# The products with the adjacency matrix in float32r, x in two parts, and due times for each operation

## The chip, the cores and the metric

The kernel runs on one core of a Trainium2 chip. The metric is the device time of one execution in microseconds. A core has five engines that run side by side and meet at semaphores: TensorE (PE, matrix products; its weight loads are listed as PEld), VectorE (DVE), ScalarE (ACT), GpSimd (POOL) and SyncE (SP), which here issues all transfers. Matrix products write to PSUM banks, all else lies in SBUF.

## The reference

The input is 32 graphs of 512 nodes: `x` (32 x 512 x 256) and `adj` (32 x 512 x 512, entries 0 and 1, ones on the diagonal), both float32. Four layers follow one another, each with a residual and a layer norm. Cut to what matters:

```python
# layer 0: attention with 8 heads, masked by adj
scores = einsum('bhqd,bhkd->bhqk', q, k) / sqrt(HD)
scores = where(adj[:, None] > 0, scores, NEG)
x = layernorm(x + einsum('bhqk,bhkd->bhqd', softmax(scores), v) @ Wo + bo)
# layer 1: aggregate, then two dense layers of 512
h = (1.0 + eps) * x + einsum('bnm,bmd->bnd', adj, x)
x = layernorm(x + relu(h @ W1 + b1) @ W2 + b2)
# layer 2: aggregate, then two dense layers of 1024 with RMS norm and silu
agg = epsilon * x + einsum('bnm,bmd->bnd', adj, x)
h = agg @ W1 + b1
x = layernorm(x + silu(rmsnorm(h) * rms_weight) @ W2 + b2)
# layer 3: Laplacian of adj, scaled by the degrees
s_out, s_in = rsqrt(sum(adj, 1)), rsqrt(sum(adj, 2))
L = eye - s_out[:, :, None] * adj * s_in[:, None, :]
pre = xn @ W_self + einsum('bij,bjf->bif', L, xn) @ W_neigh
x = layernorm(x + softplus(pre))
```

So adj enters three large products with 256 columns of features: one in layer 1, one in layer 2 and one in layer 3.

## The kernel before

One graph is worked at a time in tiles of 128 nodes (NT = 4 tiles) and 128 features (DC = 2). `graph(b)` does not issue instructions. It describes each operation of graph b to a planner (`Order`): the engines that can do it with an estimated cost on each (in nanoseconds), the keys that it reads and writes, the buffers that it holds. When all 32 graphs are described, `emit` gives each operation a due time, which is the graph's number times `PERIOD` plus a value from an early and a late pass over one graph and a lead for its stage (`LEAD`), and then simulates the engines: at each step the ready operation with the smallest due time goes next on its engine. The order thus found is what each engine's queue holds; operations of two or three graphs stand mixed in it. Where an operation can go to two engines (`either`, `copy_either`, `evacuate`), the planner takes the one that ends first by its estimate.

The stages of a graph, with the names used later:

- `load`: x into `y_att` (L407), adj into `ad` (L410; one buffer, so the load of the next graph waits until the last use of this one).
- `adjT`: the transposed adj, two buffers. The first graph transposes `ad` on PE into PSUM (`pt_adj`, L605) and ACT copies it out, summing the rows for `d_out` on the way (L615). The others load adj a second time in runs of 32 elements with four transfers (`load_blocks`, L595), transpose the 32x32 blocks on DVE with two instructions (L629) and let ACT sum over each of four tiles in place (L639). `bias` on DVE (L653) makes the mask for the attention.
- `xT`, `qk`, `v`, `scores`, `move`, `pv`: the attention. PE writes the scores, DVE adds the mask and takes the maximum (L808), ACT takes the exponential (L822), DVE transposes blocks (L858), and the result goes out to DRAM (`via`) and back (`pT`). In the first graph PE does these transposes too (`pt_p`, L841). `pr_r` (L970) spreads the reciprocal sums with small bfloat16 products.
- `wo`, `degree`, `ln0`: output product; ACT sums adj for `d_in` (L1102); two chains of small operations make `s_out` and `s_in`; layer norm.
- `agg1`: `set_diagonal` on DVE (L1159) puts `diag0` (the diagonal of adj) plus the self weight on adjT's diagonal; `aggregate` (L1177) makes the product: for each of 2 feature tiles and 4 node tiles a float32 product of 128 x 128 by 128 x 512 columns, into a bank `ph`.
- `w11`, `w12`, `ln1`, `agg2`, `w21`, `rms`, `w22`, `ln2`: the dense layers, and the second aggregate. In `rms` DVE scales 8 tiles of gT (L1333) and ACT takes Silu in two halves (L1348). POOL adds the squares (`ssq`, L554).
- `x3T`, `pz`: x goes out and back through DRAM for its transpose; the product with both weights of layer 3 gives `zy` (its first half the self part, its second the neighbour part, which is scaled with `s_in`).
- `lap`: 4 x 4 float32 products of adjT with 256 columns of zy into `pa_l` (L1489), and a DVE operation per tile that scales by `ns_out` and adds (L1500).
- `softplus`, `ln3`: ACT makes Abs, Exp and Ln in a tile `sp`; POOL adds; layer norm; store.

Some tags are shared buffers: `aT` (one) holds the tile `aT` between `w11` and `w12`, and later `zy`; `sq` (one) holds the squares; `y` (three) holds the residuals and `sp`; `adjT` has two.

## Time and profile before

| what | us |
|---|---|
| three runs | 3340.52, 3337.96, 3341.30 |
| median | 3340.52 |
| span of the profiled execution, first to last instruction | 3336.2 |
| PE busy in it | 3284.9 |
| DVE busy | 2672.1 |
| ACT busy | 1958.3 |
| POOL busy | 842.5 |
| transfers, mean share of the 16 DMA engines | 73.4% |

The costliest groups that touch adjT, from the table of instructions (busy us, then the mean ns of one):

| group | count | busy | one |
|---|---|---|---|
| L1177 PE, both aggregates | 512 + 512 records | 230.4 + 227.4 | 603 and 596 |
| L1489 PE, Laplacian | 1024 records | 229.2 | 382 |
| L629 DVE, block transposes of adjT | 62 | 75.5 | 1238 |
| L639 ACT, row sums | 124 | 76.5 | 618 |
| L1102 ACT, column sums | 128 | 78.7 | 616 |
| L1159 DVE, set_diagonal | 64 | 43.3 | 676 |

PE's records overlap, since products are pipelined: the mean of one is longer than the distance between two. The distance is what counts, and it is read from a run of them in the order of time (length over number). One float32 product leaves two records. The transfers are listed by the instruction that issued them, with the time to landing.

### The profile page before, as it was taken

Reading aid. Unit: us, or ns where it says so; the run is one execution under the profiler, and the core shown is the slowest. Engines: PE = TensorE matmul, PEld = TensorE weight load, DVE = VectorE, ACT = ScalarE, POOL = GpSimd, SP = SyncE. Lnnn points to the kernel's source line nnn. Section 1 sums busy time; section 2 is a strip of 40 time slices with the busy share of each in tenths; the row PEclk is TensorE's granted clock in tenths of the full one; section 3 lists DMA queues with packets and bytes.
Section 4 is the critical chain, followed back from the end, with each engine's and each line's share of the span. In section 5 each row is a group of like instructions: output and inputs, shape, how many; then the busy total and the mean of one; then the engine's idle time right before and its main releaser. Section 6 shows DMA issues by size and latency. Waiting matters only on the chain.

```text
span 3336.2 us, 54850 instructions
## 1 busy us (share of the span) xinstructions
PE 3284.9 (98%) x19624; PEld 1980.4 (59%) x19624; DVE 2672.1 (80%) x6195; ACT 1958.3 (59%) x4062; POOL 842.5 (25%) x611
## 2 busy tenths in 40 slices
PE   8999999999999999999999999999999999999997
PEld 5456665566665566655566655666555666556654
DVE  8878887788887888887888878888878878778855
ACT  6555666566665656665665656666656556566534
POOL 1222222222222222222222222222222222222221
PEclk9999999999999999999999999999999999999999
DMA  6878777777777777786777877777877778777720
GB/s 152 249 223 230 199 207 221 200 227 211 203 216 226 199 219 210 208 227 196 222 212 204 214 226 198 223 203 213 223 210 211 217 199 216 224 197 217 197 44 26
DMA packets 768193, 677.21 MB, mean 203 GB/s; under 512 B 540208, under 2 KB 592304, under 8 KB 736176
## 3 DMA queue, kind: packets, MB, share of 16 engines
q1 hardware_dynamic: 767920, 673.71, 73.4%
q8 instruction: 155, 2.54, 0.3%
q14 instruction: 118, 0.97, 0.1%
HBM read 380.52 MB, written 293.08 MB: 202 GB/s over the span
## 4 chain that ended last, share of the span: by engine, by line
PE 93%; DVE 2%; DMA 2%; ACT 1%; SPq 1%; issue 0%; POOL 0%; POOLq 0%; DVEq 0%; ACTq 0%
PE po L998 22%; PE ph L1177 13%; PE pg L1194 12%; PE sc L784 8%; PE po_att L900 7%; PE pa_l L1489 7%; PE pa L1194 6%; PE pq L711 6%; PE pz L1443 6%; PE pv L752 3%; DMA via<-pq 1%; SPq L595 1%; ACT pq L822 1%; DVE pq L858 0%; DVE pq L808 0%
## 5 line engine op out<-in xcount | busy, mean ns | idle before, releaser
L822 ACT ACTIVATE pq<-pq,mx 128x512 f32<-128x512 f32 x1024 | 729.1, 713 | 307.0 <-DVE mx L808 279.1
L808 DVE CUSTOM_DVE_ANT_0 pq<-sc,bias 128x512 f32<-128x512 f32 x1024 | 664.6, 682 | 97.8 <-PE sc L784 87.6
L858 DVE STREAM_TRANSPOSE pq<-pq 128x2048 f32<-128x2048 f32 x248 | 569.7, 2298 | 148.8 <-ACT pq L822 147.7
L1194 PE MATMUL pg<-hT,w 128*128 128x512 f32 x1024 | 469.9, 598 | 0.2 <-DVE zy L1454 0.2
L998 PE MATMUL po<-w,gT 128*128 128x256 f32 x2048 | 448.6, 379 | 6.8 <-ACT gT L1348 6.8
L554 POOL TENSOR_TENSOR ssq<-ssq,sq 128x512 f32<-128x512 f32 x218 | 277.9, 1275 | 589.3 <-ACT sq L1270 589.3
L998 PEld LDWEIGHTS po<-w,gT 128*128 128x128 f32 x2048 | 388.7, 190 | 63.9 <-ACT gT L1348 9.6
L1051 POOL TENSOR_TENSOR rstd<-ve,nhalf 128x4 f32<-128x4 f32 (+1 forms) x132 | 134.5, 1020 | 843.3 <-DVE ve L1046 842.1
L1194 PEld LDWEIGHTS pg<-hT,w 128*128 128x128 f32 x1024 | 189.3, 190 | 261.3 <-issue 223.6
L784 PE MATMUL sc<-kT,qT 32*128 32x512 f32 x2048 | 291.9, 640 | 0.3 <-DVE mx L808 0.3
L900 PEld LDWEIGHTS po_att<-pT,v 128*32 128x32 f32 x8192 | 219.6, 110 | 49.8 <-DVE zy L1454 21.2
L1443 PE MATMUL pz<-wsn,xnT 128*128 128x512 f32 x512 | 240.2, 595 | 5.2 <-DVE s_in L1118 3.3
L900 PE MATMUL po_att<-pT,v 128*32 128x128 f32 x8192 | 237.3, 273 | 2.1 <-DMA pT<-via 2.1
L1177 PE MATMUL ph<-adjT,y_att 128*128 128x512 f32 x512 | 230.4, 603 | 0.0
L998 PE MATMUL po<-w,aT 128*128 128x256 f32 x1024 | 229.5, 382 | 0.0
L1489 PE MATMUL pa_l<-zy,adjT 128*128 128x256 f32 x1024 | 229.2, 382 | 0.0
L1194 PE MATMUL pa<-hT,w 128*128 128x512 f32 x512 | 228.3, 599 | 0.0
L1177 PE MATMUL ph<-adjT,y 128*128 128x512 f32 x512 | 227.4, 596 | 0.0
L998 PEld LDWEIGHTS po<-w,aT 128*128 128x128 f32 x1024 | 192.0, 190 | 48.4 <-issue 22.0
L1489 PEld LDWEIGHTS pa_l<-zy,adjT 128*128 128x128 f32 x1024 | 192.1, 190 | 26.4 <-issue 0.9
L822 ACT ACTIVATION_READ_ACCUMULATOR pq<-pq,mx 128x1 f32 x1024 | 192.3, 188 | 0.0
L1270 ACT ACTIVATE sq<-gT 128x512 f32<-128x512 f32 x224 | 140.0, 625 | 88.4 <-POOL ssq L554 44.2
(166 smaller groups left out, 4685.1 us busy)
## 6 DMA issues: line engine op xcount, KB each, us to landing
via<-pq SPq DMA_DIRECT2D x992, 256.0 KB, 5.0
pT<-via SPq DMA_DIRECT2D x248, 1024.0 KB, 6.7
adj<-in_adj_dram SPq DMA_DIRECT2D x32, 1024.0 KB, 8.3
adjT<-in_adj_dram SPq DMA_DIRECT2D x124, 256.0 KB, 6.7
y_att<-in_x_dram SPq DMA_DIRECT2D x32, 512.0 KB, 4.3
xT<-in_x_dram SPq DMA_DIRECT2D x124, 128.0 KB, 4.0
x3d<-y SPq DMA_DIRECT2D x31, 512.0 KB, 2.9
xnT<-x3d SPq DMA_DIRECT2D x124, 128.0 KB, 7.2
```

The costliest lines, as they stand in the source:

```text
L554: lambda: nc.gpsimd.tensor_tensor(dst(), dst(), src(), ALU.add), {},
L711: nc.tensor.matmul(pq(), lhsT=w[:, c, m * P : (m + 1) * P], rhs=xT[:, c, :], start=(c == 0), stop=(c == DC - 1),)
L784: nc.tensor.matmul(sc[:, j, :], lhsT=qT[hp, g, t * P : (t + 1) * P], rhs=kTs[g][hp, :], start=True, stop=True,)
L808: lambda t=t, j=j, sc=sc, row=row: nc.vector.tensor_tensor_reduce(out=row(), in0=sc[:, j, :].rearrange("p (a n) -> p a n", a=4), in1=bias[ ...
L822: lambda t=t, j=j, row=row: nc.scalar.activation(row(), row(), AF.Exp, bias=mx[:, t, j : j + 1], scale=-1.0, accum_out=rs[:, g, t, j : j + 1],
L858: lambda pq=pq: nc.vector.transpose(pq().rearrange("p a j c s -> p (a j c s)"), pq().rearrange("p a j c s -> p (a j c s)"),),
L900: nc.tensor.matmul(po[j * HD : (j + 1) * HD, t * P : (t + 1) * P], lhsT=v[:, c, h * HD : (h + 1) * HD], rhs=pTs[t][:, :, j, c, :], start=( ...
L998: nc.tensor.matmul(po[:, i * D : (i + 1) * D], lhsT=lhs[:, k, t * P : (t + 1) * P], rhs=w[:, k, :], start=(i == 0 and k == 0), stop=(i == ...
L1177: nc.tensor.matmul(ph(), lhsT=xin[:, m, c * P : (c + 1) * P], rhs=adjT[:, m, :], start=(m == 0), stop=(m == NT - 1),)
L1194: nc.tensor.matmul(pa(), lhsT=w[:, c, m * P : (m + 1) * P], rhs=hT[:, c, :], start=(c == 0), stop=(c == DC - 1),)
L1443: nc.tensor.matmul(pz(), lhsT=xnT[:, c, t * P : (t + 1) * P], rhs=wsn[:, c, :], start=(c == 0), stop=(c == DC - 1),)
L1489: nc.tensor.matmul(pa[:, at], lhsT=adjT[:, m, t * P : (t + 1) * P], rhs=zy[:, m, D : 2 * D], start=(m == 0), stop=(m == NT - 1),)
```

## The change

Six things change at once.

1. `adjT` becomes a float32r tile for every graph. The operand on the other side (x1, x2, or the scaled neighbour half of zy) is split by `parts_of` into a float32r copy (high) and the rest (low), also float32r: one operation each on DVE or ACT, and on DVE or POOL. `aggregate` then makes two products for each that it made before; the Laplacian's product has both parts side by side as 512 columns, and the two halves of the bank are scaled and added.
2. Whether the float32r copies of adj and of its changed diagonals are exact is checked on the chip: differences on POOL, their absolute sums on ACT into `inexact`, and after the last graph one sum and one small product into `found`. A register is loaded from it; if it is not zero, a loop does all graphs again in float32 (`general=True`, one graph at a time, in the order as written).
3. adj is transposed on PE in all graphs, not only in the first; the second load of adj and DVE's block transposes of it go.
4. The due times are a list with one number for each operation, in three lists (first graph, graphs between, last graph); the early and late passes go. A handicap of 1000 ns is added to DVE wherever an operation can go to several engines.
5. Work is moved between engines: the column sums of adj come early, into a scratch tile; the two degree chains become one on tiles twice as wide; `set_diagonal` is an addition on POOL and a copy on ACT or DVE; half of the RMS scalings go to POOL, and their Silu runs by tile; layer norm's last step can go to POOL.
6. Buffers: `y_att` takes one of the three `y` buffers, and its load waits for the residual `r2` of the graph before; `sp` goes, and softplus works in place in `zy`; the parts of x (`hl`) use the buffer of `aT`; the scratch tiles of the checks use that of `sq`.

The core of the diff:

```diff
-PERIOD = 68064
-LEAD = {
-    "adjT": 136800, "agg1": -11000, "agg2": -29700, "degree": 92400, "diag": 77700,
...
+AHEAD = 3
+PERIOD = 117877
+DUE = {
+    "first": [
+        -953, -1983, -977, -2779, -2566, -630, -2955, -2775, -1468, -707, -1979, -879, -867, -503,
...
+    HANDICAP = {"PE": 0, "DVE": 1000, "ACT": 0, "POOL": 0, "SP": 0}
...
-            for o, d in zip(lst, dues[len(lst)]):
-                keys[o.n] = b * period + d - (self.HASTE if b == max(by_b) else 0)
+            due = DUE["first" if b == 0 else "last" if b == max(by_b) else "middle"]
+            for o, d in zip(lst, due, strict=True):
+                keys[o.n] = b * period + 100 * d
...
-        y = tmp([P, NT, D], "y_att", 2)
+        y = tmp([P, NT, D], "y", 3, "y_att")
...
-            [], [(y, t) for t in range(NT)],
+            [("r2", b - 1)], [(y, t) for t in range(NT)],
...
-        adjT = tmp([P, NT, N], "adjT", 2)
...
-            for q in range(4):
-                op(
-                    [("SP", 2500, lambda q=q: load_blocks(adjT(), adj[b], q), {"issue": 1250})],
...
+        adjT = tmp([P, NT, N], "adjT", 2, dtype=F32 if general else F32R)
...
+        def differs(c, t, k, cost):
+            act(
+                cost,
+                lambda: nc.scalar.activation(t(), t(), AF.Abs, accum_out=inexact[:, b, c : c + 1]),
+                [], k + [("inexact", b, c)],
+            )
+
+        for m in range(NT):
+            pt = bank("pt_adj")
...
+            pe(460, tr_adj, [(ad, t) for t in range(NT)], [(pt,)], adjT, d_out)
+            act(
+                860,
+                lambda m=m, pt=pt: nc.scalar.activation(
+                    adjT[:, m, :], pt(), AF.Identity, accum_out=d_out[:, m : m + 1]
+                ),
+                [(pt,)], [(adjT, m), (d_out, m)],
+            )
...
+            if not general:
+                pool(
+                    1280,
+                    lambda t=t, same=same: nc.gpsimd.tensor_tensor(
+                        ad[:, t, :], ad[:, t, :], same().bitcast(F32), ALU.subtract
+                    ),
+                    [(same,)], [(ad, t)],
+                )
...
+        def set_diagonal(selfI, self_k, c):
+            t = tmp([P, NT, P], "sq", 1, "diag")
+            pool(
+                1280,
+                lambda: nc.gpsimd.tensor_tensor(
+                    t(), diag0(), selfI.unsqueeze(1).to_broadcast([P, NT, P]), ALU.add
+                ),
+                [(diag0,), (self_k,)], [(t,)],
+            )
+            copy_either(lambda: diagonal(adjT()), t, [(t,)], allT)
...
+        def parts_of(src, src_k, dst, dst_k):
+            high = lambda e: e.tensor_copy(dst(0), src())
+            low = lambda e: e.tensor_tensor(dst(1), src(), dst(0).bitcast(F32), ALU.subtract)
+            op(
+                [
+                    ("DVE", 300, lambda: high(nc.vector), {"port": 1}),
+                    ("ACT", 420, lambda: nc.scalar.copy(dst(0), src()), {}),
+                ],
+                src_k, [dst_k(0)],
+            )
+            op(
+                [
+                    ("DVE", 350, lambda: low(nc.vector), {}),
+                    ("POOL", 690, lambda: low(nc.gpsimd), {}),
+                ],
+                src_k + [dst_k(0)], [dst_k(1)],
             )
...
+            if not general:
+                hl = tmp([P, 2, NT, D], "aT", 1, "hl", dtype=F32R)
+                for t in range(NT):
+                    parts_of(
+                        lambda t=t: xin[:, t, :], [(xin, t), ("lapped", b - 2)],
+                        lambda r, t=t: hl[:, r, t], lambda r, t=t: (hl, r, t),
+                    )
...
+                            for r in range(1 if general else 2):
+                                src = xin[:, m] if general else hl[:, r, m]
+                                nc.tensor.matmul(
+                                    ph(),
+                                    lhsT=src[:, c * P : (c + 1) * P],
+                                    rhs=adjT[:, m, :],
...
+        whole = C2 if general else C2 // 2
+        if whole < C2:
+            pb_s = tmp([P, N], "sq", 1, "pb_s")
+            evacuate(pb_s, pb, [(pb,)], [(pb_s,)])
         for m in range(C2):
+            if m >= whole:
+                pool(
+                    1280,
+                    lambda m=m: nc.gpsimd.tensor_tensor(gT[:, m, :], gT[:, m, :], pb_s(), ALU.mult),
...
+                    nc.tensor.matmul(
+                        pa[:, 0:D] if general else pa(),
+                        lhsT=adjT[:, m, t * P : (t + 1) * P],
+                        rhs=zy[:, m, D : 2 * D] if general else yhl[:, m].rearrange("p r d -> p (r d)"),
...
+    any_found = nc.values_load(found[0:1, 0:1], min_val=0, max_val=1)
+    with tc.If(any_found != 0):
+        with tc.For_i(0, B, 1) as i:
+            one = Order()
+            parts = [v[bass.ds(i, 1)].rearrange("o n d -> (o n) d") for v in (x, adj, out)]
+            graph(0, one, *parts, general=True)
```

## The prediction, made before the changed kernel was run

> **What bounds the kernel now.** I read the page's busy shares and its forty slices first.
>
> ```profile
> PE 3284.9 (98%) x19624; PEld 1980.4 (59%) x19624; DVE 2672.1 (80%) x6195; ACT 1958.3 (59%) x4062; POOL 842.5 (25%) x611
> ...
> PE   8999999999999999999999999999999999999997
> ...
> PEclk9999999999999999999999999999999999999999
> ```
>
> TensorE (PE) works in every slice at the full granted clock; only the first and last slices dip. A busy PE may still wait, so I looked at one graph's period in the table of stretches and in the chain of waits:
>
> ```profile
> 578.67:680.32 101.65, 101.65 (x610) 61.20 (x609) 82.74 (x193) 61.19 (x128) 26.56 (x20) 1.00 0.79 213
> 1304.00:1405.66 101.66, 101.66 (x610) 61.22 (x609) 82.67 (x192) 61.32 (x128) 26.57 (x19) 1.00 0.78 213
> ```
>
> The columns are length, then busy time of PE, weight loads, DVE, ACT and POOL. The steady period is 101.66 us, PE has no hole in it, and DVE has 19 us, ACT 40 us, POOL 75 us to spare. 32 periods are 3253 us; the other 83 us of the 3336.2 us span are its two ends. The chain of the second stretch is PE alone:
>
> ```profile
> 1312.20 7.07 PE ph L1177 x16
> ...
> 1342.04 0.45 PE pr_r L970 x8
> 1342.49 6.92 PE ph L1177 x16
> ...
> 1377.57 7.00 PE pa_l L1489 x32
> ```
>
> So a microsecond taken from PE here shortens the period, until another engine or a buffer stops it. The three products with adj (aggregate twice, the Laplacian once) cost 7.07 + 6.92 + 7.00 = 20.99 us.
>
> **The change, part by part.**
>
> *The products.* A float32 product leaves two PE records: ph's 8 products are 16 records of 0.442 us, pa_l's 16 products are 32 records of 0.219 us at half the columns. So a record streams at two steps a column, a float32 product at four. pr_r's bf16 products, one record each, take 0.45/8 = 0.056 us for 128 columns: one step. No float32r product is in the trace. After the change each stage has 16 products of 512 columns (two parts times eight in aggregate; 16 with both parts side by side in the Laplacian), 48 a graph. Bounds for one: 512 bf16-like columns, 4 x 0.056 = 0.225 us; one record of float32, 0.442; a whole float32 product, 0.884. I take 0.222, between the bf16 figure and the 0.219 of a record with equally many steps: splitting x into parts that are exact in a narrower format means one pass over a shorter mantissa, which the bf16 row is nearest to. The weight load must hide: it is 0.190 us for pa_l's records and does so under 0.219. 48 x 0.222 = 10.66 us; saved 10.33 a graph, 330.6 us in all.
>
> *adj transposed on PE.* The first graph already does this; the other 31 get 16 more transposes each. The trace has both a warm and an early stretch:
>
> ```profile
> 7.86 3.28 PE L605 MATMUL pt_adj<-ident,adj 128*128 128x128 f32 x16 [1.18 <-DMA adj<-in_adj_dram]
> ...
> 51.72 3.28 PE L841 MATMUL pt_p<-ident,pq 128*128 128x128 f32 x28
> ```
>
> Per transpose 0.205 us early, 0.117 amid other work. I take the second, since the steady part is like it: 31 x 16 x 0.117 = 58 us (bound 102).
>
> "TensorE: Matmul & The Clock Gate" of the Trainium skill, Part 4, speaks against this edit: about 0.275 us for a transpose inside a kernel, and transposes do not hold the clock up. By that figure the edit would cost 136 us, an estimate of that page's; the rows above say less than half, with the clock granted in full, and the trace decides.
>
> What leaves with it: four adj loads a graph in 32-element runs (6.7 us to landing, 9 us of SP's queue at 1384.61) and two DVE transposes (2 x 1.238 us). DMA and DVE are off PE's path, so this gives nothing directly. The four accumulating ACT passes (618 + 188 ns) become four like them out of PSUM (592 + 193): nothing.
>
> *Side work, all charged at nothing on PE's path.* Worked per graph from nearest rows, against a new period of 101.66 - 10.33 + 1.87 = 93.2:
> - DVE 82.8, less 2.48 (adjT transposes), 1.35 (set_diagonal 2 x 676 ns), 2.96 (four of eight RMS scalings at 741 ns), 0.64 (four small degree ops): 75.4. The twelve highs, twelve lows, four scalings and four additions of the Laplacian would add about 13.5 at the 407 to 479 ns of 256-column rows, if all went there: 88.9. The planner's new 1000 ns handicap sends most elsewhere.
> - ACT 61.3, plus highs and scalings 16 x 0.507, two checks of 1024 columns at 0.98 + 0.19, two of 512 at 0.81, two diagonal copies at 0.618, the RMS copy 0.58 and the split Silu 0.6: about 75.7.
> - POOL 26.6, plus 12 passes of 512 columns at 1.275 (adj check, diagonals, RMS half) and 16 of 256 at about 0.62 (half of that row), less one power of 1.02: about 50.9.
>
> None reaches 93.2. Their cover is PE's own work; if a static order leaves PE waiting on them, the wait adds in full. For this I allow 0.5 us a graph, 16 us; it could be nothing or, by the second rival, several us a graph.
>
> "SBUF — State Buffer" of the Trainium skill, section "SBUF: two separate sides", states that a DVE operation with two SBUF inputs and a GpSimd operation lock each other out for the whole instruction. In this trace the bias operation lies beside long POOL passes at 419 ns as without them, while POOL is busy a quarter of the time; nothing here shows it at half. An estimate by the rule, 0.55 x 0.64 us of waiting before some 16 DVE operations, is 5.6 us of DVE a graph, still under 93.2.
>
> *Added waits.* The load of x for graph b now waits until the residual r2 of b-1 is issued (1342 in the stretch shown; bo's addition and then wo at 1398 want it): over 50 us of cover for a 4.3 us load. Behind it on SP's queue stand via, pT and adj loads, and those feed scores and the transposes; the order places it after its release, so I charge nothing. PE's transposes wait for adj's load (8.3 us to landing); its single buffer is now freed after two checks instead of one ACT pass, with a period to land in. A late load would stop everything behind it on PE. Hi/lo and the aT buffer: hl, aT and zy share one buffer, occupied some 69 of 101.66 us by the present times (hl's two spans included); the sq buffer is likewise shared. Both have slack.
>
> *The end.* The flag's register load and the branch come after all work: nothing in the trace is like it; bounds 0 and 15 us (twice a 7.9 us tiny load), I take 5, a small load's landing (4.2 to 8). The general path's body is skipped if nothing is found; 0/1 entries and small diagonal integers are exact in any of these formats. New due values at both ends: the 83 us there may move by 15 either way; 0.
>
> Sum: 3336.2 - 330.6 + 58 + 16 + 5 = 3084.6 us of span; the median run lies 4.3 above the profiled span, so 3089.
>
> **Rivals.**
>
> *Another resource sets the period (0.20).* adjT has two buffers:
>
> ```profile
> L1489 PE MATMUL pa_l<-zy,adjT x32: 379/379/462, 1377.4 to 1384.2; 128*128 128x256 f32 x32
> ...
> L595 SPq DMA_DIRECT2D adjT<-in_adj_dram x4: 593/1316/5905, 1384.6 to 1392.4; - x4
> ```
>
> The load for a later graph starts the moment one Laplacian ends, and that copy lives until another Laplacian two periods on, about 200 us. At 93.2 it must live only 186. For: longer chains (high, low, check, two-step diagonal, scale and add), and DVE and ACT at 81%. Against: load plus transpose took 1384.6 to 1406, about 21 us, and PE's version needs some 5; the products in between shrink too. If it holds the period at 97, 32 x 3.8 above 93.2 gives 3195; at 101, 3320.
>
> *One mechanism on the slow side (0.07): float32r streams at two steps a column,* as the 4-byte transposes do (pt_p, one record of 128 columns, 0.117, against 0.056 for bf16). 48 x 0.442 = 21.2 gains nothing against 20.99; the transposes, waits and end remain: 3340.5 + 7 + 58 + 16 + 5 = 3427. It decides from 0.40 us a product, where 48 of them plus 1.87 equal the old 20.99. At four steps it would be 48 x 0.884 = 42.4, some 4105. Against: then two parts would buy nothing.
>
> *The change doesn't do what it says (0.02):* a check finds a part inexact, and the float32 path repeats all 32 graphs, one after the other, each at least 101.66 us: over 6300.
>
> *Better (0.10):* no waits, cheap end, half of the loss at the ends regained, transposes at 0.109: under 3050.
>
> **How the numbers follow.** Forecast 0.61 (its own span 3050 to 3125), others as given. The range 3035 to 3230 leaves out about half of "better", under half of the period rival and both slow cases, near 0.19. A measurement of this kernel can't tell differences under 0.2%, 7 us. Faster: 0.61 + 0.10 + 0.18 = 0.89; the period rival's worst end gives same 0.02; slower 0.09.
>
> **What would show it.** Right: ph and pa_l records one per product, spaced about 0.217 to 0.225; steady period 93 to 94.5; pt_adj at 0.11 to 0.13 in 32 graphs; no adjT loads; PE still without holes; POOL near half busy. Wrong: spacing at 0.43; PE waits named after ACT adjT, POOL low parts or the adj load; a period over 96; or a run twice as long.

## The result, and the profile after

The changed kernel is slower: a median of 3540.61 us over four runs (3526.41 to 3541.95) against 3339.86 us (3337.96 to 3341.30) of the kernel before, a ratio of 1.0587 with a 95% interval of 1.0565 to 1.0609. The forecast was 3089 us. The profiled execution took 3526.41 us, with a span of 3524.5 us.

The busy times, two of the rows of forty slices, and the engines' shares of the chain that ended last, as the page of the changed kernel has them:

```profile
PE 3183.9 (90%) x19610; PEld 1993.0 (57%) x19610; DVE 2980.0 (85%) x6371; ACT 2137.2 (61%) x4595; POOL 1625.1 (46%) x1350
...
PE   8898999898998899998989999999989899889886
...
PEclk9899999999999999999999999999999999999998
...
PE 49%; DVE 21%; DMA 16%; SPq 6%; ACT 3%; issue 3%; POOL 2%; DVEq 0%; POOLq 0%; ACTq 0%
```

TensorE has become faster and stands more: 3183.9 us busy against 3284.9, in a span that is 188 us longer. Many slices are no longer full. The chain, 93% TensorE before, is TensorE for a half only and goes over VectorE and the DMAs for the rest. What TensorE waits for is in the table of its waits (total, times, longest):

```profile
PE sc L892 <- DVE mx L916: 83.1, 31, 3.1
PE ph L1316 <- DVE hl L1281: 60.8, 32, 3.4
PE pz L1608 <- DVE xnT L1592: 34.3, 22, 2.7
PE pm_t L1049 <- DVE sumsp L1032: 23.7, 29, 3.8
PE pm_t L1049 <- DVE rmsp L1032: 20.5, 28, 3.0
```

22 to 32 times each: the same holes in most of the 32 graphs. The largest lies between the last product of layer 1's second dense (`po<-w,aT`) and layer 2's aggregate (`ph`). This is TensorE's timeline there, start and length in us, of the kernel before:

```profile
1535.78 3.19 PE L998 MATMUL po<-w,aT 128*128 128x256 f32 x14
1538.80 3.60 PE L711 MATMUL pq<-xT,wq 128*128 128x512 f32 x8
1542.33 1.14 PE L784 MATMUL sc<-kT,qT 32*128 32x512 f32 x8
1543.40 0.26 PE L941 MATMUL pm_t<-ident_b,sumsp 128*96 128x128 bf16 x1
1543.49 1.94 PE L711 MATMUL pq<-xT,wk 128*128 128x512 f32 x4
1545.27 0.61 PE L970 MATMUL pr_r<-mT_sums,sel_r 96*128 96x128 bf16 x8
1545.72 1.51 PE L1177 MATMUL ph<-adjT,y 128*128 128x512 f32 x3
```

and of the changed kernel:

```profile
1602.55 1.14 PE L892 MATMUL sc<-kT,qT 32*128 32x512 f32 x8
1603.62 1.98 PE L819 MATMUL pq<-xT,wk 128*128 128x512 f32 x4
1608.37 1.14 PE L892 MATMUL sc<-kT,qT 32*128 32x512 f32 x8 [2.77 <-DVE mx L916]
1609.88 0.79 PE L1316 MATMUL ph<-adjT,hl 128*128 128x512 f32 x1 [0.37 <-ACT hl L1285]
...
1612.92 0.79 PE L1316 MATMUL ph<-adjT,hl 128*128 128x512 f32 x1 [2.24 <-DVE hl L1281]
```

Between the two products VectorE has to add the residual, take the statistics and normalize; now the cast and the subtraction of the split follow. Before, 6.75 us of other graphs' work on TensorE (3.60 + 1.14 + 0.26 + 1.94 + 0.61, overlapping a little) covered that chain with no idle time. In the new order 4.3 us stand there (two rows of scores and one key projection), the second row of scores has to wait until VectorE has masked the row before it (there is one buffer `sc`), which it does only after the statistics, and the chain is longer by the split. So TensorE stands 2.77 us and then 0.37 and 2.24 us more, and much the same in nearly every graph. The chain of waits around this place (some of its pieces, start and length) is VectorE's from the end of `po` to the second product of `ph`, 10.3 us:

```profile
1595.52 7.12 PE po L1106 x32
...
1602.66 0.69 DVE y L1120
...
1605.55 0.69 DVE pq L916
...
1608.95 2.69 DVE hl L1281 x2
...
1612.92 4.34 PE ph L1316 x11
```

After this place the granted clock falls. The table of stretches gives length, busy time of PE, PEld, DVE, ACT and POOL, then the clock:

```profile
1594.00:1608.30 14.30, 11.60 (x54) 7.30 (x52) 12.49 (x31) 6.28 (x16) 1.57 (x2) 1.00 0.74 205
1608.30:1620.00 11.70, 8.97 (x34) 5.29 (x35) 10.27 (x18) 6.19 (x17) 4.19 (x3) 0.71 0.86 273
1620.00:1640.00 20.00, 18.26 (x53) 7.32 (x53) 15.55 (x25) 11.90 (x26) 9.20 (x7) 1.00 0.89 254
```

Over the whole run the clock is at half in 44 periods, 320 us together; before, in 3, 20 us. VectorE, finally, is stretched where GpSimd works beside it:

```profile
1608.87 2.92 DVE L1281 TENSOR_TENSOR hl<-y,hl 128x256 fp32r<-128x256 f32 x2
1608.97 2.54 POOL L1252 TENSOR_TENSOR y<-y,b_r 128x1024 f32<-128x1024 f32 x1 [0.69 <-DVE hl L1280]
```

Two subtractions of about 0.42 us took 2.92 us, about as long as GpSimd's addition. That addition is the residual of the layer, which the kernel before makes too; 29 subtractions of the split lay beside it and took 2 us longer each, 59 us together. Counting for every VectorE instruction what it took over the fastest tenth of its kind, this came to 69.9 us before and 342.8 us after.

TensorE's span can be taken apart from its records: the gaps between its products are idle time, the two ends lie before its first product and after its last, half of what it was busy at half clock is the clock's surcharge, and the rest is work at full clock.

| us | span | idle | two ends | surcharge of the half clock | work at full clock |
|---|---|---|---|---|---|
| before | 3336.2 | 34.8 | 16.5 | 3.7 | 3281.3 |
| after | 3524.5 | 317.0 | 23.6 | 118.3 | 3065.6 |
| difference | +188.3 | +282.2 | +7.1 | +114.6 | -215.7 |

The products did get cheaper. Which of the three suspects (holes that the order makes, the clock, GpSimd's interference) carries the loss, and whether it is the added work or its place, is what the experiments ask. Runs of the changed kernel itself lay between 3526 and 3542 us, so differences below some 15 us are not read.

### The profile page after: what moved, and what is told of

The parts are those of the page before. It is cut to its first block, busy times and chain, and to the rows that moved or that the text cites. A ratio compares the mean times of both kernels' runs of the same rounds, so it can differ in the third digit from the quotient of the medians.

```text
span 3524.5 us, 56358 instructions
## 1 busy us (share of the span) xinstructions
PE 3183.9 (90%) x19610; PEld 1993.0 (57%) x19610; DVE 2980.0 (85%) x6371; ACT 2137.2 (61%) x4595; POOL 1625.1 (46%) x1350
## 4 chain that ended last, share of the span: by engine, by line
PE 49%; DVE 21%; DMA 16%; SPq 6%; ACT 3%; issue 3%; POOL 2%; DVEq 0%; POOLq 0%; ACTq 0%
PE po L1106 16%; DMA via<-pq 10%; PE ph L1316 8%; PE pz L1608 6%; DVE pq L966 6%; PE pa L1340 5%; DMA xnT<-x3d 4%; SPq L978 4%; PE po_att L1008 4%; PE pg L1340 4%; DVE pq L916 3%; PE sc L892 2%; POOL rr L671 2%; PE pq L819 2%; DMA xT<-in_x_dram 2%
## 5 line engine op out<-in xcount | busy, mean ns | idle before, releaser
L1106 PE MATMUL po<-w,gT 128*128 128x256 f32 x2048 | 464.4, 382 | 6.8 <-ACT gT L1503 4.7
L1316 PE MATMUL ph<-adjT,hl 128*128 128x512 f32 x1024 | 341.8, 492 | 71.6 <-DVE hl L1281 60.8
L892 PE MATMUL sc<-kT,qT 32*128 32x512 f32 x2048 | 304.2, 661 | 83.1 <-DVE mx L916 83.1
L1316 PEld LDWEIGHTS ph<-adjT,hl 128*128 128x128 f32 x1024 | 240.9, 240 | 181.4 <-DVE hl L1281 77.2
L1608 PEld LDWEIGHTS pz<-wsn,xnT 128*128 128x128 f32 x512 | 98.2, 197 | 182.8 <-issue 108.5
L892 PEld LDWEIGHTS sc<-kT,qT 32*128 32x128 f32 x2048 | 83.2, 186 | 206.6 <-issue 198.5
L753 POOL TENSOR_TENSOR adj<-adj,same 128x512 f32<-128x512 f32 x128 | 162.5, 1270 | 70.9 <-ACT same L744 70.8
L930 ACT ACTIVATION_READ_ACCUMULATOR pq<-pq,mx 128x1 f32 x1024 | 192.5, 188 | 0.0
```

Source lines behind the costliest of these rows:

```text
L753: lambda t=t, same=same: nc.gpsimd.tensor_tensor(ad[:, t, :], ad[:, t, :], same().bitcast(F32), ALU.subtract),
L892: nc.tensor.matmul(sc[:, j, :], lhsT=qT[hp, g, t * P : (t + 1) * P], rhs=kTs[g][hp, :], start=True, stop=True,)
L930: lambda t=t, j=j, row=row: nc.scalar.activation(row(), row(), AF.Exp, bias=mx[:, t, j : j + 1], scale=-1.0, accum_out=rs[:, g, t, j : j + 1],
L1106: nc.tensor.matmul(po[:, i * D : (i + 1) * D], lhsT=lhs[:, k, t * P : (t + 1) * P], rhs=w[:, k, :], start=(i == 0 and k == 0), stop=(i == ...
L1316: nc.tensor.matmul(ph(), lhsT=src[:, c * P : (c + 1) * P], rhs=adjT[:, m, :], start=(m == 0 and r == 0), stop=(m == NT - 1 and (general or ...
L1608: nc.tensor.matmul(pz(), lhsT=xnT[:, c, t * P : (t + 1) * P], rhs=wsn[:, c, :], start=(c == 0), stop=(c == DC - 1),)
```

## The experiments

### GpSimd's load

The first two leave instructions out of the changed kernel and keep its order. e1 leaves out the exactness check, six GpSimd and four ScalarE passes a graph; e2 also GpSimd's half of the RMS scalings and its additions of the Laplacian's low product.

```diff
-    lambda t=t, same=same: nc.gpsimd.tensor_tensor(ad[:, t, :], ad[:, t, :], same()..., ALU.subtract),   # e1, e2
+    lambda: None,
...
-    lambda m=m: nc.gpsimd.tensor_tensor(gT[:, m, :], gT[:, m, :], pb_s(), ALU.mult),              # e2
+    lambda: None,
```

> The changed kernel in the very same order, with the instructions of the exactness checks left out: six POOL passes of 512 columns (1.27 us each, 7.6 us a graph) and four accumulating ACT passes. The text says that this leaves out the check. Two theories. Collision theory: POOL's longer work (50.8 us a graph instead of 26.6) holds up DVE operations that work from SBUF to SBUF, such as L1281 at a mean of 1014 ns where 421 is the middle one, and the late DVE results open the holes on PE, which then also runs at half clock for 320 us of the run. Then this run gains 80 to 150 us (3380 to 3450), and the time by which DVE's operations exceed their own short form, 343 us over the run, falls by a fifth or more. Order theory: the order laid down by the due list leaves PE without work whatever POOL does; then the time stays within 40 us of 3530.

> As the run before, and in the same order, with POOL's four RMS scalings and POOL's or DVE's four additions in the Laplacian left out too (POOL some 15 us a graph less than in the changed kernel; the results of both steps are left out). Collision theory: the gain goes on, 3300 to 3400, the clock is granted above 0.97, and the stretched DVE operations shrink further. Order theory: at most 60 us below the changed kernel.

Measured: 3475.6 and 3451.4 us; VectorE's stretching falls from 342.8 to 284.8 and 192.5 us, the time at half clock stays (340 and 321 us), and so do the waits of the scores (82.1 and 82.8 us) and for the low parts (56.9 and 54.4 us). What does go with the check is TensorE's wait at `pm_t`, from 44 to 6 us. The check is worth 65 us, the rest of GpSimd's new work 24. Both times lie between the two theories: above what interference as the cause would have given, with the clock still near 0.95, and below what order alone would (the 65 us are more than 40, the 89 us together more than 60). Neither run takes away GpSimd's residual addition, so at the largest hole the subtraction stays stretched, in e2 still beside 25 additions (48 us).

The counterpart loads the kernel before. e3 gives GpSimd 32 additions of two 256-column operands a graph, 0.742 us each, which nothing waits for; e4 gives it nearly as much work that only writes, two memsets beside each mask.

```diff
+    def extra():                                                                   # e3, for each of the 32 masks
+        nc.gpsimd.tensor_tensor(scr, wsn[:, 0, 0:256], wsn[:, 1, 0:256], ALU.add)
...
+    def extra():                                                                   # e4
+        nc.gpsimd.memset(scr, 0.0)
+        nc.gpsimd.memset(scr, 0.0)
...
-    lambda t=t, j=j, sc=sc, row=row: nc.vector.tensor_tensor_reduce(
+    lambda t=t, j=j, sc=sc, row=row: extra() or nc.vector.tensor_tensor_reduce(
```

> The kernel before, in its own order, with one more POOL operation for each of its masks: an addition of two 256-column inputs from SBUF into a scratch tile that nobody reads (32 a graph, some 0.73 us each, about 23 us a graph, so that POOL's load is near that of the changed kernel). Collision theory: DVE's SBUF-to-SBUF rows (L1069 407 ns, L1058 159, L1537 1133, L1159 676) get means longer by a third to double, holes open on PE, the time goes up by 40 to 150 us. Order theory: POOL and DVE have room (26.6 and 82.8 of 101.7 us), so the time stays within 20 us of 3340 and the rows keep their means.

> As the run before, but the added POOL work only writes: two memsets of 256 columns for each mask. Collision theory in the form that reading matters: rows with two inputs from SBUF (L1159, L1537, L1058) keep their means, and the time stays nearer to 3340 than in the run with reads. Collision theory in the form that any POOL work blocks: as much slower as the run with reads. Order theory: within 20 us of 3340.

Measured: 3360.6 us with GpSimd 1586.1 us busy, nearly as much as in the changed kernel, and 3342.1 us with 1458.7. The reading load stretches VectorE by 162.7 us in all against 69.9, the writing load hardly (92.2). Of the four rows named ahead of e3, one tripled (159 to 519 ns), one grew by a tenth (676 to 740) and two kept their means, so neither theory had the rows right. Yet before's order gives up only 20 us for it, and TensorE stays at 98%. Interference is real, but what it costs depends on the order it meets.

### The holes and the clock

e5 and e9 fill the two holes with bfloat16 products whose results are overwritten. e5 put the first eleven ahead of the key projection, e9 behind it, directly before the waiting scores (the diff is e9's).

```diff
+    def keep_warm(to):
+        nc.tensor.matmul(to, lhsT=ident_b, rhs=sel_r.rearrange("p x e -> p (x e)")[:, 0:512], start=True, stop=True)
...
+    late.fill += [one.ph] * 11      # before the fourth row of scores, into the next aggregate bank
+    two.fill += [two.ph] * 7        # before the second group of aggregate products
```

> The changed kernel with 19 extra bfloat16 products of 512 columns a graph, whose results are overwritten: 11 before the key projection that precedes the wait of the scores for VectorE (2.77 us a graph) and 8 before the second group of aggregate products, that waits for the low parts of the split (1.6 to 2.1 us a graph). They do nothing but fill two holes. Theory clock (the holes cost twice: once as waits, once more because the granted clock falls to half after them): time at half clock falls from 320 us to under 100 us, and the time to 3400 to 3470 us. Theory order (the half clock only eats time that TensorE would have waited anyhow): half-clock time falls as well, but the waits behind grow and the time stays over 3500 us.

> The changed kernel with 18 extra bfloat16 products of 512 columns a graph, put directly into the two holes: 11 between the key projection and the scores that wait for VectorE, 7 ahead of the aggregate products that wait for the low parts, each into the bank of the aggregate product that comes next and overwrites them. Unlike the fill ahead of the key projection (3614 us, TensorE then waited 71 us more for the ACT casts behind the later projection) it delays no result that another engine waits for, except by what the products outlast the holes. Theory clock: time at half clock falls from 320 us to under 120 us, and the time to 3400 to 3480 us. Theory order: the half clock ate time that TensorE would have waited for VectorE anyhow, and the time stays within 3500 to 3570 us.

e5 took 3613.7 us: the key projection came 2.4 us later, its eviction on ScalarE too, and the cast of the split stood behind that eviction (`ph` waits for ScalarE's `hl` 71 us). It tested its own placing. e9 delays nothing of the sort, and its timeline at the place shows the first hole closed:

```profile
1615.43 1.14 PE L908 MATMUL sc<-kT,qT 32*128 32x512 f32 x8
1616.50 1.98 PE L831 MATMUL pq<-xT,wk 128*128 128x512 f32 x4
1618.53 2.32 PE L630 MATMUL ph<-sel_r,ident_b 128*128 128x512 bf16 x10
1621.24 1.14 PE L908 MATMUL sc<-kT,qT 32*128 32x512 f32 x8 [0.39 <-DVE mx L933]
```

The time at half clock fell from 320 to 207 us and its surcharge from 118 to 86 us, but the time rose to 3573.6 us, 4 us over what the order theory allowed: TensorE still waits 281 us, now more for the low parts (73.1 us) and for `hT` (27.3 us). The fill is 116 us of new work on TensorE; 36 of them took the place of idle time and 32 of surcharge, the rest made the run longer than the profiled one (by 47 us). So the clock's theory got no support here. It was not tested to the end either: two thirds of the half clock were left where it wanted under 120 us, and in e14 below less half clock does come with a shorter time.

e8 swaps VectorE's order at the hole: the four masks before the four pairs of statistics.

```diff
+    at = max(out.index(stats[0]), scores + 1)
+    out[at:at] = masks
```

> The changed kernel with one swap in VectorE's order: the four masks that the waiting scores need run before the four pairs of normalization statistics instead of after them. If the hole is a fault of the order that a swap mends, the scores wait 1.8 us less a graph or more and the time falls by 60 to 150 us, to 3390 to 3480 us. If VectorE as a whole is what is short there, the wait of the scores (83 us) shrinks but that of the aggregate products for the low parts (61 us) grows by as much, the half clock stays, and the time is 3510 to 3570 us.

```profile
1640.03 1.14 PE L911 MATMUL sc<-kT,qT 32*128 32x512 f32 x8
1641.11 1.98 PE L838 MATMUL pq<-xT,wk 128*128 128x512 f32 x4
1643.92 1.14 PE L911 MATMUL sc<-kT,qT 32*128 32x512 f32 x8 [0.83 <-DVE mx L935]
1649.59 0.79 PE L1335 MATMUL ph<-adjT,hl 128*128 128x512 f32 x1 [4.53 <-ACT hl L1304]
```

The scores' wait shrank from 2.77 to 0.83 us and the aggregate's grew to 4.53 us; 3612.1 us, worse than either theory had it. At this place VectorE owes TensorE two things at once, and TensorE has too little else to do.

### The load of one engine

e7 leaves out the products with the low parts, e10 two of VectorE's eight in-place transposes of a graph, e11 the low parts altogether.

```diff
-    for r in range(1 if general else 2):
+    for r in range(1):                                                # e7, e11
...
+    (lambda: None) if g == 0 and t in (1, 2) else                     # e10
     lambda pq=pq: nc.vector.transpose(
...
-    ("DVE", 350, lambda: low(nc.vector), {}),
+    ("DVE", 350, lambda: None, {}),                                   # e11, and on GpSimd
```

> The changed kernel without the products with the low parts (the low parts are still made; only the high parts are multiplied): 24 products of 0.231 us a graph less on TensorE, 177 us in all. If TensorE still sets the time of the changed kernel, the time falls by about that, to 3340 to 3400 us. If the order and VectorE set it, TensorE only waits longer, and the time stays above 3460 us.

> The changed kernel without two of VectorE's eight in-place transposes of a graph (2.30 us each, second and third row of the first heads; the attention weights of these rows stay untransposed), everything else in its place: 4.6 us of VectorE a graph less, 143 us in 31 graphs, in the stretch where the masks, the normalization and the split all want VectorE. Counterpart of the run that took 5.5 us of TensorE a graph away and gained 67 us. Theory 'VectorE's stretch is in the loop that sets the period': the scores' wait for the masks (83 us) or the low parts' (61 us) shrinks and the time falls by 90 to 200 us, to 3340 to 3450 us, more than the 143 us where the half clock goes too. Theory 'TensorE sets it': under 40 us less, 3500 to 3540 us.

> The changed kernel without the low parts: neither made (on VectorE and GpSimd) nor multiplied. Against the run without the low products alone (3473 us) it has only VectorE's and GpSimd's subtractions less: 12 to 16 a graph, 0.4 us each on VectorE where GpSimd lets it be and up to 2.9 us where not. If these subtractions in VectorE's stretch carry much of the loss: 3300 to 3400 us, with VectorE's stretching down by 60 us or more. If the order loses the time whatever is made in it: 3430 to 3475 us.

| run | left out | time | against 3540.6 |
|---|---|---|---|
| e7 | 177 us of TensorE | 3473.5 | -67 |
| e10 | 135 us of VectorE (2980.0 to 2844.6 busy) | 3523.2 | -17 (-3 against the profiled run) |
| e11 | as e7, and VectorE 85, GpSimd 150 us | 3464.6 | -76 |

TensorE's largest wait in e7:

```profile
PE sc L892 <- DVE mx L916: 209.1, 61, 4.7
```

It has grown from 83.1 us; idle time rose from 317 to 394 us and the half clock's from 320 to 404. Of some 178 us of work that TensorE was spared, 77 came back as idle time and 47 as surcharge of the clock. Both forecasts that took VectorE's stretch as the pace failed as well. But e10 did not reach the chain of 10.3 us: the two transposes that it leaves out stood before the residual additions and behind the last subtraction, and the waits stayed, as its table has them:

```profile
PE sc L892 <- DVE mx L916: 83.2, 32, 3.0
PE ph L1317 <- DVE hl L1282: 64.0, 33, 3.4
```

So e10 shows that VectorE's load as a sum is not scarce, and says nothing of its chain at this place. e11 does shorten that chain, stretched subtractions included, and gains 9 us over e7, which is below what is read here: `sc` still waits 179.5 us for the masks. No sum of work of TensorE or VectorE is the bound of the changed kernel. Work passes from one to the other within a graph, and each waits in turn. ScalarE and the transfers, which have 3% and 16% of the chain that ended last, were not tried.

### The work, or its place

e6 puts only the price of the new products into the kernel before, in its own order: 48 float32r products on one constant tile for the 24 float32 ones (counted at 512 columns; the Laplacian's are twice as many of 256), with small one-column products on the real tiles so that the waits stay.

```diff
-    nc.tensor.matmul(ph(), lhsT=xin[:, m, c * P : (c + 1) * P], rhs=adjT[:, m, :], ...)
+    if c == 0: nc.tensor.matmul(ph[0:1, 0:1], lhsT=xin[:, m, 0:1], rhs=adjT[:, m, 0:1], ...)
+    for r in range(2):
+        nc.tensor.matmul(ph(), lhsT=fixed, rhs=fixed.unsqueeze(1).to_broadcast([P, 4, P]), ...)
```

> The kernel before in its own order, the 24 float32 products of a graph replaced by the 48 float32r products of the change, on one constant float32r tile (x, adj and the split are left out of these products; 12 products of one column a graph stay on the real tiles, so that the waits stay). It has the price of the new products alone, without the split on VectorE and GpSimd, the transposes and the new order. Theory 'the prices were right': 48 x 0.231 = 11.1 us against 20.99 us a graph, 32 x 9.9 = 317 us less, 20 to 80 us for the one-column products: 3045 to 3110 us with TensorE above 95%. Rival 'before's order has no room either' (other engines set the period as soon as TensorE is faster): over 3200 us, with waits of TensorE for VectorE that the kernel before didn't have, and a granted clock below 0.98.

3231.0 us: the rival's time, with new waits as it had them, but with a clock of 0.994 where it wanted one below 0.98, and with TensorE at 97%, as the first theory had it. The products took more than that theory's 11.1 us a graph (14.5, waits between them included). Counted from each product's start to the next, the three stages took 464.6 us and the one-column products 46 us, against 679.0 us before: 168 us less. The time fell by 109; the rest came back as waits that the kernel before didn't have:

```profile
PE 3123.2 (97%) x20392; PEld 1939.4 (60%) x20392; DVE 2659.7 (82%) x6196; ACT 1947.8 (60%) x4062; POOL 843.0 (26%) x611
...
PE pv L755 <- issue: 20.5, 27, 0.8
PE sc L787 <- DVE mx L811: 20.0, 20, 1.8
```

So even in the order that had kept TensorE without a hole, only about two thirds of what TensorE saves reaches the end.

e13 and e12 add the change's other work to e6, still in before's order: a cast and a subtraction-sized operation for each of the 12 tiles of the split (in place), the Laplacian's second eviction and addition, the diagonal on GpSimd; e12 also 16 transposes a graph. e14 and e15 vary e12: e14 makes the Laplacian's second addition after the fused one on each tile, e15 leaves second eviction and addition out.

```diff
+    def parts_of(_, x, name, t):
+        nc.vector.tensor_copy(x, x) if t < 2 else nc.scalar.copy(x, x)
+        low = nc.vector if name != "lap" and t < 3 else nc.gpsimd
+        low.tensor_tensor(x, x, x, ALU.add)
...
+    for t in range(NT): nc.tensor.transpose(pq[:, t * P : (t + 1) * P], ident, ident)     # e12, e14, e15
...
-    lambda ...: low_sum(t, pa[:, at]) or nc.vector.scalar_tensor_tensor(...)                 # e12, e13
+    lambda ...: low_sum(nc.vector.scalar_tensor_tensor(...), t, pa[:, at])                   # e14
```

> The kernel before in its own order with the change's work put into it: the 48 float32r products a graph on a constant tile (x and adj left out of them), 16 transposes a graph on TensorE (of a constant, ahead of the four q and k projections), a cast and a subtraction-sized operation for each of the 12 tiles of the split, in place, shared out as in the change (6 casts on VectorE and 6 on ScalarE, 6 of the others on VectorE and 6 on GpSimd; they double x), the second eviction and addition of the Laplacian, the diagonal on GpSimd. Not in it: the checks, the RMS halves on GpSimd; adj still comes transposed by DMA and VectorE. Theory order: it costs the 58 us of transposes and 20 to 50 us of waits over 3231 us: 3280 to 3335 us, still under the kernel before. Theory parts (the work itself, not where the order puts it, makes the loss): over 3420 us, with the scores' and aggregates' waits and the half clock of the changed kernel.

> The same without the 16 transposes. It parts their price from the split's in before's order. Theory order: 3230 to 3290 us; 40 to 60 us under the run with them. Theory parts: over 3370 us.

> The run with all the change's work in before's order (3419 us), with one thing put elsewhere: the second eviction and addition of the Laplacian come after the first on each tile instead of ahead of it, so that VectorE doesn't wait in its queue for ScalarE and GpSimd (TensorE stood 3.2 us a graph, 86 us, at the value projection behind that). The same instructions run. Theory order (where the work is queued makes the loss): the 3.2 us hole and most of the half clock (176 us) go: 3270 to 3340 us. Theory parts (its amount does): over 3390 us.

> The same without the Laplacian's second eviction and addition, with the split of the 12 tiles and the transposes: what the split itself costs in before's order. Theory order: 3260 to 3330 us, within 20 us of the run above. Theory parts: over 3360 us.

Measured: e12 3419.0, e13 3378.8, e14 3342.0, e15 3295.9 us. By their times e12 and e13 speak for the parts theory, if barely (3419, just short of "over 3420", and 3379 for "over 3370"). But the trace of e13 shows a hole at TensorE's value projection, which e12 shares, and where it comes from:

```profile
1700.38 0.48 ACT L1495 ACTIVATE zy<-pa_l,ns_out 128x256 f32<-128x256 f32 x1 [1.93 <-PE pa_l L1518]
...
1700.93 0.74 POOL L1499 TENSOR_TENSOR zy<-zy 128x256 f32<-128x256 f32 x1 [2.24 <-ACT zy L1495]
1701.70 0.48 DVE L1529 SCALAR_TENSOR_TENSOR zy<-pa_l,ns_out,zy 128x256 f32<-128x256 f32 x1 [0.87 <-POOL zy L1499]
...
1704.12 1.23 DVE L691 STREAM_TRANSPOSE xT<-xT 128x1024 f32<-128x1024 f32 x1
...
1705.45 1.85 PE L761 MATMUL pv<-wv,xT 128*128 128x256 f32 x4 [3.20 <-issue]
```

VectorE stands in its queue for ScalarE and GpSimd, tile after tile; behind it waits the transpose of x, and TensorE for that. The placing is the experiment's own. The wait in e12 and, with the same instructions in the other order, in e14 (one line from each table of waits):

```profile
PE pv L763 <- issue: 86.1, 27, 3.2
```

```profile
PE pv L763 <- issue: 42.2, 27, 1.6
```

One move in a queue, no work more or less, is worth 77 us, and brings e14 to 2 us over the order theory's band. By TensorE's account 28 of the 77 us are idle time and 52 surcharge of the half clock, which lasted 174 us in e12 and 63 in e14: here the clock after the hole weighs more than the hole. e15 lies inside its own, but 46 us under e14 where 20 were expected: the Laplacian's second addition has a price even where it stands well. So an imitation of the change's work, without the check and the RMS halves on GpSimd, fits into before's order at before's time. It gains nothing there either.

e16 makes that move in the changed kernel, e17 also leaves out the check.

```diff
-    add_to(lambda t=t: zy[:, t, 0:D], lambda t=t: zy[:, t, D : 2 * D], ...)
+    op([("POOL", 690, lambda t=t, later=later: later.append((nc.gpsimd, t)), {}), ...
...
-    lambda t=t, pa=pa: nc.vector.scalar_tensor_tensor(...)
+    lambda t=t, pa=pa, later=later: [nc.vector.scalar_tensor_tensor(...)] + [low_sum(*x) for x in later]
```

> The changed kernel, whole, with the one move that gained 77 us in before's order: on each tile of the Laplacian the addition of the low product comes after VectorE's fused scale-and-add, not ahead of it, so that VectorE no longer waits in its queue for ScalarE's eviction and GpSimd's addition. Theory order: TensorE's waits at the transposes of adj and the normalizers (pm_t, 44 us), which stand behind this place on VectorE, shrink, and the time falls by 20 to 90 us, to 3440 to 3510 us. If the due list already kept VectorE clear of it: within 15 us of 3530.

> The same without the instructions of the exactness check (6 GpSimd and 4 ScalarE passes a graph left out), which alone gained 65 us. If the two losses are separate places of the queues, they add: 65 us and the gain of the run above below 3530 us. If they are one (GpSimd late with the addition because of the checks), less than that.

3505.7 and 3472.5 us: 35 us gained (`pm_t`'s two waits fell from 44 to 30 us), and only 3 more on top of e1, too little to read, where two separate places would have added. The check's price and this place are largely one thing. That it is GpSimd coming late with the additions fits the waits at `pm_t`, which the check's work alone takes from 44 to 6 us, but was not shown apart. Put in a row:

| what is in it | us | step |
|---|---|---|
| before (3347.5 beside e6, 3338 to 3341 beside the others) | 3340 | |
| float32r products, before's order (e6) | 3231 | -109 |
| and split, transposes, diagonal (e15) | 3296 | +65 |
| and the Laplacian's second addition, well placed (e14) | 3342 | +46 |
| the changed kernel without check, addition moved (e17) | 3472 | +130 |
| and the check (e16) | 3506 | +33 |
| the changed kernel | 3541 | +35 |

The step of 130 us is between two kernels with nearly the same instructions in two orders. It isn't the order alone: e17 has half of the RMS scalings on GpSimd (with the Laplacian's additions worth 24 us by e2), its split reads and writes real parts in one more buffer and its transposes wait for the real adj, while e14 multiplies and transposes constants and still loads adj a second time. These were not parted further.

## Why the prediction was wrong, point by point

**The prices of TensorE's work were near.** A stage of the changed kernel at full clock:

```profile
1581.78 4.07 PE L1316 MATMUL ph<-adjT,hl 128*128 128x512 f32 x16
```

Sixteen float32r products in 4.07 us; the median from one to the next is 0.235 us, where I took 0.222. Transposes of adj follow one another in 0.109 us (median; mean 0.157 with the evictions between), where I took 0.117. With the starts of their runs counted, and the half clock taken out, the products of the three stages came to 12.2 us a graph where I had 10.66, and the transposes to 72 us where I had 58. The rival that had float32r at two steps a column is refuted, though the time overshot even its 3427. Work at full clock fell by 215.7 us, where my two terms give 272.6.

**The step that failed** is the one on waits: "Their cover is PE's own work; if a static order leaves PE waiting on them, the wait adds in full. For this I allow 0.5 us a graph, 16 us". The measured term is 282 us of idle time, and 115 us of half clock along with it, which the sum didn't have at all. The span came out 440 us over my sum: 266 of them are these waits, 115 the clock, 57 TensorE's work and 2 its ends. I compared the sum of each engine's work with the period ("None reaches 93.2") and took it that a load below the period is covered. Two of the loads came out at or below what I had, GpSimd with 51 us a graph (forecast 50.9) and ScalarE with 66 (75.7). VectorE's did not: with its stretching it was busy for 93 us (75.4 to 88.9), all of the period that I forecast, so the comparison failed there on its own terms. It isn't what set the period of some 108 us, in which VectorE had 15 to spare. Cover is a matter of what stands in TensorE's queue between two dependent steps, and that the change rewrote with its list of due times. The kernel's own planner, by its own costs, leaves TensorE some 270 us idle under the new list and some 40 under the old one, and ends at 3287 us against 3317, so that even it had only 30 us to gain. The list was in the diff, and I charged the whole of it with a moved end.

**"So a microsecond taken from PE here shortens the period"** holds for two thirds in before's order (109 of 168 us, e6). An engine that is 98% busy hides how near the next waits are.

**VectorE and GpSimd.** I weighed "SBUF — State Buffer" of the Trainium skill, section "SBUF: two separate sides", against one row (the bias operation at 419 ns) and put it aside. That row has one input where the rule as I gave it speaks of two, so it could not decide. The page also limits the rule for two inputs to GpSimd operations that read SBUF. The two subtractions that took 2.92 us beside a 2.54 us addition agree with the exclusion, and e3 against e4 shows it for a GpSimd load that reads and hardly for one that only writes, as the page says. My estimate by the rule was 5.6 us of VectorE a graph; the stretching grew by (342.8 - 69.9) / 32 = 8.5 us. That alone didn't make the loss: nearly as much load cost before's order 20 us, and e2, with over half of the added stretching gone, is still 110 us slower than the kernel before.

**The other rivals.** TensorE never waited for a buffer of adjT: the transposes of adj waited 6.4 us for a load, once, and 4.7 us for an eviction. Another resource that sets the period was the nearest case, with the wrong resource, a wrong price (3195 to 3320) and on the wrong side. The general path was not taken.

**What stays open:** which loop across the engines sets the period of some 108 us in the changed kernel, and how the step of 130 us divides between the order and what e14 leaves out. The runs exclude TensorE's load and VectorE's load as causes by themselves. For the clock they don't: less of it gained nothing in e9 and came with most of the gain in e14. An order of the same instructions that leaves no holes was not found and not run.

## What to carry to other kernels

When a change rewrites a hand-made or searched order, do not carry over the old trace's "no holes": list, for each chain that leaves the bounding engine and comes back, what that engine has in its queue meanwhile, and compare it with the chain's length. A chain made longer (here by a cast and a subtraction) needs more cover even where every engine has time to spare. And before filling a hole, ask what the next instruction on each in-order queue waits for: moving one addition behind its neighbour gained 77 us in before's order and 35 in the changed kernel, filling holes with idle products lost 33. Where a planner made the order, read its own forecast first: here it had 30 us to offer.

## What the runs showed of the hardware that was not expected

- A hole shorter than 3 us is enough for the clock. In graph after graph the granted clock fell to a half at the end of the 2.77 us hole or up to 2.6 us later, mostly for 6.8 or 10.2 us; five falls for 3.4 us came just behind holes of 1.7 to 2.2 us. It is not certain: after holes of 2.65 us (at 338.70) and 2.80 us (at 3430.52) no fall followed. "TensorE: Matmul & The Clock Gate" of the Trainium skill, Part 1, gives free-running windows of 3413 ns, and these lengths are 1, 2 and 3 of them; but it asks for a whole idle window, and here a hole of 2.77 us did it.
- Filling a hole with idle products lowered the time at half clock from 320 to 207 us and gained nothing (3540.6 to 3573.6 us).
- GpSimd stretches VectorE by reading: 162.7 us of stretching for additions, 92.2 us for memsets, 69.9 us with neither.
- A float32r product of 512 columns leaves one record and takes 0.235 us; a float32 one leaves two of 0.442 us each.
